# A graph layer on one core: a ring of twenty gather buffers, and 44 instead of 40 columns a step copied on the chip

## The chip, the cores and the metric

The kernel runs on one core of a Trainium2 chip. A core has five engines that run side by side: TensorE (PE, with its weight load shown apart as PEld), VectorE (DVE), ScalarE (ACT), GpSimd (POOL) and SyncE (SP, which here issues DMAs). Each engine has a sequencer that takes its instructions in program order; engines meet through semaphores. The metric is the device time of one execution in microseconds (us), lower is better.

## The reference, cut to what matters

A graph of 12500 nodes (64 features) and 212500 edges (32 features), the edges sorted by destination. For each edge a small network is applied to the source node, the destination node and the edge; messages are summed by destination; a second network updates each node, followed by a residual and a layer norm.

```python
def _L0_gnn_ref(nodes, row, col, edge_features, mW1, mb1, mW2, mb2, uW1, ub1, uW2, ub2):
    msg_in = jnp.concatenate([nodes[row], nodes[col], edge_features], axis=-1)
    messages = _mlp(msg_in, mW1, mb1, mW2, mb2)
    aggregated = jax.ops.segment_sum(messages, col, num_segments=nodes.shape[0])
    upd_in = jnp.concatenate([nodes, aggregated], axis=-1)
    return _mlp(upd_in, uW1, ub1, uW2, ub2)
x = _layernorm(x + _L0_gnn_ref(x, src, dst, edge_attr_32, ...), axis=-1)
```

`src` is random, so `nodes[row]` is a gather of 212500 rows of 256 bytes. `_mlp` is a matrix product, a ReLU and a second product.

## The kernel before, in words

Edges are worked on in 554 groups (`G`) of 384 edges, three tiles of 128. Since edges are sorted, all destinations of a group lie in a window of 32 consecutive nodes. All features of all nodes lie on the chip, transposed, in `own_xc` (64 partitions of features, one column a node, and a row of counts). The loop at the end of `ordered` runs over the groups; its body is one step `k`, and a step works on three groups at once:

- `turn(k)`: TensorE transposes the three gathered tiles of group k, together with their one-hot window matrix, into PSUM (line 341); ACT copies them to `own_st` (line 351), where the edge features have been loaded by SP.
- `hidden(k - 2)`: TensorE multiplies `own_st` with the weights `own_wm` (line 366), ACT applies the ReLU (line 377).
- `sums(k - 4)`: TensorE multiplies by the one-hot matrices, giving sums over the window of hidden vectors (line 394) and of edge counts (line 399). VectorE adds them into `agg` (line 406) and into the counts' row of `own_xc` (line 407), at a column held in a register.

TensorE's work of a step is issued in one run that waits once. PSUM buffers alternate, so a step's transposes need what ACT and VectorE did two steps before.

Source rows come in two ways. POOL gathers them from memory with one indirect DMA a tile (line 149, `gather`), `AHEAD` groups ahead of the loop, into a ring of `RING = AHEAD + 4` buffers `own_s`. A buffer may be written again when the transposes of the group before in it are done; before, both groups of a pair wait for the transposes of the pair's second group. But the first tile of some groups (those in `COPIED`) isn't gathered: its 128 columns are copied one by one out of `own_xc`, by VectorE and ACT, straight into `own_st` (`fetch`, lines 503 and 505; each copy is 64 partitions x 4 bytes). `COPIED` holds one group as soon as 128 more columns have been copied, from step 18 (`BEGIN`) up to ten steps before the last group. To copy a column, its address has to be in a register of the engine: a load instruction (line 490, `TENSOR_LOAD`) brings 8 or 12 addresses from `index` into registers at a time, then the copies follow. Addresses come in blocks of eight steps (`SPAN`), loaded by SP (`indexes`, line 467) and scaled on VectorE (`addresses`, line 473).

Other work on VectorE: `onehot(k + 2)` (line 329) each step; `places` once in four steps (a register load of four window starts, line 301, and four copies to `xw`, line 308); `windows` once in four steps (TensorE line 315, four copies to `own_wm`, line 320); and once in about 22.7 steps, when 512 nodes have all their sums, an `update`, cut into stages one step apart: TensorE and ACT apply the second network (lines 424 to 437), VectorE adds (428, 439), takes the statistics (443, 444) and normalizes (451, 454), SP stores.

The order on each engine is the program's order. VectorE, before, in a step: (places) - (update) - agg add - counts' add - (wm copies) - one-hot - load of 8 - 8 copies - load of 12 - 12 copies.

The lines that set the sizes:

```python
AHEAD = 4
RING = AHEAD + 4
VCOLS = (8, 12)
ACOLS = (12, 8)
COLS = sum(VCOLS + ACOLS)
SPAN = 8
```

The functions that the diff touches:

Of the kernel before, what the change touches and what calls it, by code (L numbers as in the profile page):

```python
# [15 lines left out]
ALU = mybir.AluOpType  # L16
ET = mybir.EngineType
# [6 lines left out]
D = 64  # L24
# [7 lines left out]
GE = TG * P  # L32
G = (E + GE - 1) // GE
SB = 4
AHEAD = 4
RING = AHEAD + 4
BLOCKS = 3
NW = 2 * SB
# [7 lines left out]
SHORT = 10  # L46
TIMES = 4
BEGIN = 18
CHECKED = 8
VCOLS = (8, 12)  # L50
ACOLS = (12, 8)
COLS = sum(VCOLS + ACOLS)
SPAN = 8


def tiles_of(g):

    n = min(GE, E - g * GE)
    return [min(P, n - j * P) for j in range((n + P - 1) // P)]
# [49 lines left out]
def ordered(ctx: ExitStack, tc: tile.TileContext, a, own, ok):  # L109
# [3 lines left out]
    nc = tc.nc  # L113
# [9 lines left out]
    xc = own.xc[: D + 2]  # L123
# [7 lines left out]
    loads, places_by, copy_by, relu_by, sums_by, wm_by, turn_by = ({} for _ in range(7))  # L131
# [3 lines left out]
    def after(first, *others):  # L135

        tc.declare_no_dep(first.ins, group="quiet", reason="waits for the last of a step")
        for i in others:
            tc.add_manual_dep(
                first.ins, i.ins.name,  # L140
                mybir.DependencyInfo(mybir.DependencyClass.Sync, mybir.DependencyReason.DATA),
                reason="the kernel's own rings",
            )
        return first

    def gather(g):
        s = own.s[g % RING]
        loads[g] = [
            nc.gpsimd.indirect_dma_start(  # L149
                out=s[:p, j, :D], out_offset=None, in_=x[:, :],  # L150
                in_offset=bass.IndirectOffsetOnAxis(
                    ap=src_sb[:p, g * TG + j : g * TG + j + 1], axis=0),
            )
            for j, p in enumerate(tiles_of(g)) if j or g not in columned
        ]
        for i in loads[g]:
            after(i, *([turn_by[g // 2 * 2 + 1 - RING]] if g >= RING else []))


    iota_i = const.tile([P, W], F32, name="iota_i")  # L160
# [3 lines left out]
    make_identity(nc, ident_t)  # L164
    for g in range(AHEAD):
        gather(g)
# [55 lines left out]
    for f, (g0, g1) in zip(firsts_f, halves):  # L222
        part = dlc[:, g0 * TG : g1 * TG].rearrange("p (g j) -> p g j", j=TG)
# [18 lines left out]
    agg = const.tile([P, NP], F32, name="agg")  # L242
# [49 lines left out]
    def columns(g):  # L292
        t, c = own.st[g // SB % BLOCKS], (g % SB) * GE
        return t, c, sum(tiles_of(g))
# [92 lines left out]
    def sums(g, ps):  # L387
        h, s = own.h[g % NH], own.s[g % RING]
        sizes = tiles_of(g)
        sg = ps[2][:, : TIMES * W].rearrange("p (t w) -> p t w", w=W)  # L390
        counted = ps[2][0:1, TIMES * W :][:, :W]
        did = []
        for j, p in enumerate(sizes):
            did.append(nc.tensor.matmul(  # L394
                sg, h[:p, j, :],
                s[:p, j, D:].unsqueeze(1).to_broadcast([p, TIMES, W]),
                start=j == 0, stop=j == len(sizes) - 1))
        for j, p in enumerate(sizes):
            did.append(nc.tensor.matmul(counted, own.one[:p], s[:p, j, D:],  # L399
                                        start=j == 0, stop=j == len(sizes) - 1))  # L400

        def add(step):
            sums_by[g] = step
            at = bass.ds(starts.pop(g), W)
            return [
                after(nc.vector.tensor_tensor(agg[:, at], sg[:, 0, :], agg[:, at], ALU.add), step),  # L406
                after(nc.vector.tensor_tensor(xc[D : D + 1, at], counted,  # L407
                                              xc[D : D + 1, at], ALU.add), step),
            ]

        return did, [*relu_by[g], *copy_by[g]], add

# [49 lines left out]
    def indexes(i):  # L462

        n = min(SPAN * COLS, P * len(COPIED) - i * SPAN * COLS)
        if n > 0:
            indices[i] = ixp.tile([1, SPAN * COLS], I32, name="index")
            nc.sync.dma_start(indices[i][:, :n], a["src_copied"][:, i * SPAN * COLS :][:, :n])

    def addresses(i):

        if i in indices:
            t = indices[i][:, : min(SPAN * COLS, P * len(COPIED) - i * SPAN * COLS)]
            nc.vector.tensor_scalar(t, t, 4.0, float(own.at), ALU.mult, ALU.add)

    def fetch(k):

        i, n = divmod(k - BEGIN, SPAN)
        if i < 0:
            return
        if n == 0:  # L480
            indexes(i + 1)
        if n == SPAN - 2:
            addresses(i + 1)
        c0 = (k - BEGIN) * COLS
        for engine, count in [*((ET.DVE, c) for c in VCOLS), *((ET.Activation, c) for c in ACOLS)]:
            count = min(count, P * len(COPIED) - c0)
            if count <= 0:
                return
            b = c0 - i * SPAN * COLS
            _, v = nc.values_load_multi_w_load_instructions(  # L490
                indices[i][0:1, b : b + count], engines=[engine],
                min_val=own.at, max_val=own.at + 4 * (N - 1),
                skip_runtime_bounds_check_because="a source is one of the nodes",
            )
            for q, at in zip(range(c0, c0 + count), v):
                g, c = COPIED[q // P], q % P
                t, first_c, _ = columns(g)
                o = t.bitcast(U8)[:D, 4 * (first_c + c) : 4 * (first_c + c + 1)]
                x_at = xc_bytes[:D, bass.ds(at - own.at, 4)]
                by = columns_by.setdefault(g, {})  # L500
                new = engine not in by
                if engine == ET.DVE:
                    by[engine] = nc.vector.tensor_copy(o, x_at)  # L503
                else:
                    by[engine] = nc.scalar.activation(o, x_at, AF.Copy)  # L505
                after(by[engine], *([hidden_by[g - BLOCKS * SB]] if new else []))
            c0 += count

    waiting = [(closes, update(base, p, n)) for base, p, n, closes in PLAN]
    now = []  # L510
# [13 lines left out]
    def step(*work):  # L524


        parts, used = [], []
        for part, g in work:
            ps, old = own.ps[g % 2], users[part][g % 2]
            parts.append((part, g, *part(g, ps)))  # L530
            used += old
        did = [i for p in parts for i in p[2]]
        after(did[0], *used, *(i for p in parts for i in p[3]))
        copies = None
        for part, g, *_ in parts:
            if part is sums:
                for b in [b for b in xws if (b - 1) * SB <= g][:1]:
                    last, copies = windows(b, own.ps[g % 2][2][:, (TIMES + 1) * W :][:, :H])
                    did.append(last)
        for i in did[:-1]:  # L540
            tc.no_tile_sem_insts.add(i.ins.name)
            tc.add_to_no_dep_group("quiet", i.ins)
        for part, g, _, _, follow in parts:
            if part is sums:
                step_update(g)
            users[part][g % 2] = follow(did[-1])
            if part is sums and copies:
                copies()
                users[part][g % 2] += [wm_by[b * SB + i] for i in range(min(SB, G - b * SB))]
# [6 lines left out]
    windows(0, ups.tile([H, CH], F32, name="u_ps")[:, :H], False)[1]()  # L556
    indexes(0)
    made = summed = 0

    for k in range(G):  # L560
        if k < BITS:
            bit(k)
        if k == CHECKED:
            addresses(0)
            combined()
            ordered_edges()
            early.close()
            up = ctx.enter_context(tc.tile_pool(name="upd", bufs=2))
        if k % SB == 2:
            inputs(k // SB + 2)  # L570
        if k % SB == 1:
            places(k // SB + 1)
        if k < G - SHORT:
            step((turn, k), *([(hidden, k - 2)] if k > 1 else []),
                 *([(sums, k - 4)] if k > 3 else []))
            made, summed = max(0, k - 1), max(0, k - 3)
        else:

            step((turn, k))
            for _ in range(2):  # L580
                if summed < made:
                    step((sums, summed))
                    summed += 1
            for _ in range(2):
                if made <= k:
                    step((hidden, made))
                    made += 1
        onehot(k + 2)
        fetch(k)
        if k + AHEAD < G:  # L590
            gather(k + AHEAD)
    while summed < G:
# [332 lines left out]
```

## Time and profile before

| | us |
|---|---|
| median of 3 runs | 1899.2 (1896.05 to 1899.49) |
| profiled execution | 1895.48 |
| its span, first to last instruction | 1893.5 |
| POOL busy | 1417.6 |
| VectorE busy | 1492.9 |
| ACT busy | 1550.7 |
| TensorE busy | 1361.4 |

The page gives, for a group of instructions, the line of the kernel, the engine, the operation, what it writes and reads, how many there were, then busy time and the mean duration of one in ns, then the idle time of the engine just before them and what ended most of it. "issue" as the end of idle time means that the engine waited for nothing that the profile shows, so the cause lies in its sequencer. Register loads, address arithmetic and waits are done by the sequencer and are not counted as busy; rows marked DVEq or ACTq are such. An idle time of an engine that doesn't set the pace costs nothing. The granted TensorE clock was 0.969 of full speed on average.

### The profile page before, as it was taken

What the parts mean: (1) busy time and instruction counts of PE and PEld (TensorE: products, weight loads), DVE (VectorE), ACT (ScalarE), POOL (GpSimd) and SP (SyncE); (2) the same over time, 40 slices, a digit from 0 to 9 for tenths busy, and PEclk for the clock granted to TensorE, in tenths of its full rate; (3) what the DMA queues carried; (4) which work ended last, traced back from release to release, by engine and by line L of the source; (5) the groups of instructions that cost most, each with busy time, mean ns of one, the idle gap of its engine ahead of it and who ended that gap; (6) DMA issues with size and microseconds to landing.
All of it is one profiled execution on the core that took longest, in us unless ns stands there. A gap on an engine that the chain in (4) does not pass through costs nothing. (4 is left out here: it accounts for less than half of the span.)

```text
span 1893.5 us, 58044 instructions
## 1 busy us (share of the span) xinstructions
PE 1361.4 (72%) x12209; PEld 1193.4 (63%) x12209; DVE 1492.9 (79%) x13761; ACT 1550.7 (82%) x11818; POOL 1417.6 (75%) x1504
## 2 busy tenths in 40 slices
PE   3776777677777777677676776877767767767777
PEld 3666666666666666666665666666666656666665
DVE  3578888778888788887888878878888887888873
ACT  3489889888888888988988888889888888898882
POOL 7777777777777777777777777777777777777774
PEclk9999999999999999999999999999999999999999
DMA  6322222222222222222222222222222222222221
GB/s 136 73 46 45 46 48 44 50 43 48 46 45 48 47 43 50 45 46 44 48 50 43 48 46 45 46 48 44 50 44 47 47 48 44 47 44 50 44 47 29
DMA packets 68440, 92.50 MB, mean 49 GB/s; under 512 B 30893, under 2 KB 38350, under 8 KB 68078
## 3 DMA queue, kind: packets, MB, share of 16 engines
q0 software_dynamic: 47904, 49.12, 14.7%
q1 hardware_dynamic: 19260, 39.12, 7.4%
q14 instruction: 260, 2.13, 0.4%
q8 instruction: 102, 1.67, 0.4%
q10 hardware_dynamic: 914, 0.46, 0.1%
HBM read 85.29 MB, written 3.20 MB: 47 GB/s over the span
## 5 line engine op out<-in xcount | busy, mean ns | idle before, releaser
L149 POOL DMA_INDIRECT own_s<-in_x,src_sb x1497 | 1416.8, 946 | 457.3 <-issue 407.5
L503 DVE COPY own_st<-own_xc 64x4 uint8 x10500 | 897.7, 190 | 231.0 <-issue 217.9
L505 ACT ACTIVATE own_st<-own_xc 64x4 uint8 x10492 | 1057.1, 194 | 18.2 <-issue 15.2
L341 PE MATMUL own_ps<-own_ident,own_s 128*96 128x128 f32 x1661 | 289.5, 285 | 496.0 <-DMA own_s<-in_x,src_sb 157.9
L341 PEld LDWEIGHTS own_ps<-own_ident,own_s 128*96 128x96 f32 x1661 | 169.3, 132 | 566.1 <-ACT own_h L377 240.7
L394 PE MATMUL own_ps<-own_s,own_h 128*128 128x128 f32 x3322 | 480.5, 283 | 4.1 <-ACT own_h L377 2.9
L366 PE MATMUL own_ps<-own_wm,own_st 128*128 128x128 f32 x3322 | 479.4, 283 | 0.0
L351 ACT ACTIVATE own_st<-own_ps 96x384 f32<-96x384 f32 (+2 forms) x718 | 293.2, 408 | 205.8 <-PE own_ps L399 104.7
L394 PEld LDWEIGHTS own_ps<-own_s,own_h 128*128 128x128 f32 x3322 | 432.6, 199 | 6.3 <-ACT own_h L377 4.7
L366 PEld LDWEIGHTS own_ps<-own_wm,own_st 128*128 128x128 f32 x3322 | 432.1, 199 | 1.4 <-issue 0.5
L377 ACT ACTIVATE own_h<-own_ps 128x384 f32<-128x384 f32 x553 | 263.9, 477 | 16.0 <-PE own_ps L366 16.0
L399 PE MATMUL own_ps<-own_s,own_one 128*1 128x32 f32 x3322 | 190.1, 194 | 0.0
L320 DVE COPY own_wm<-own_ps 32x128 f32<-32x128 f32 x550 | 156.9, 285 | 5.6
L399 PEld LDWEIGHTS own_ps<-own_s,own_one 128*1 128x1 f32 x3322 | 114.5, 84 | 69.4 <-issue 6.2
L329 DVE TENSOR_TENSOR own_s<-iota,dlc 128x96 f32<-128x96 f32 x554 | 142.4, 258 | 14.3 <-issue 0.2
L406 DVE TENSOR_TENSOR agg<-own_ps,agg 128x32 f32 x554 | 105.1, 190 | 59.5 <-PE own_ps L399 25.9
L407 DVE TENSOR_TENSOR own_xc<-own_ps,own_xc 1x32 f32 x554 | 101.2, 183 | 30.6 <-PE u_ps L425 11.4
L308 DVE COPY xw<-own_xc 66x32 f32 x554 | 73.0, 207 | 15.5 <-DMA own_xc<-in_xT 9.8
L315 PE MATMUL own_ps<-w1b,xw 66*128 66x128 f32 (+1 forms) x276 | 69.1, 333 | 0.0
L446 ACT ACTIVATE rstd<-mv,eps 128x4 f32<-128x4 f32 (+1 forms) x25 | 7.4, 297 | 55.3 <-DVE mv L444 55.3
L437 PE MATMUL u_ps<-u,u 128*128 128x64 f32 (+1 forms) x196 | 50.1, 399 | 0.5 <-ACT u L427 0.5
L437 PEld LDWEIGHTS u_ps<-u,u 128*128 128x128 f32 (+1 forms) x196 | 47.1, 324 | 2.2 <-ACT u L427 0.9
(62 smaller groups left out, 276.7 us busy)
## 6 DMA issues: line engine op xcount, KB each, us to landing
own_st<-in_efT SPq DMA_DIRECT2D x138, 192.0 KB
own_s<-in_x,src_sb POOLq DMA_INDIRECT x1497
xin<-in_x SPq DMA_DIRECT2D x24, 128.0 KB
out<-o SPq DMA_DIRECT2D x24, 128.0 KB
own_xc<-in_xT SPq DMA_DIRECT2D x12, 179.2 KB
index<-in_src_copied SPq DMA_DIRECT2D x65, 1.2 KB
dlc_i<-in_dst_cols SPq DMA_DIRECT2D x1, 831.0 KB
own_xc<-in_xT SPq DMA_DIRECT2D x4, 179.5 KB
```

The lines of the kernel that those rows point to most:

```text
L149: nc.gpsimd.indirect_dma_start(out=s[:p, j, :D], out_offset=None, in_=x[:, :], in_offset=bass.IndirectOffsetOnAxis(ap=src_sb[:p, g * TG + ...
L320: c = nc.vector.tensor_copy(wm[g % NW][D : D + W, :], wp[i * W : (i + 1) * W, :])
L329: places_by[g] = nc.vector.tensor_tensor(own.s[g % RING][:, :, D:], iota.unsqueeze(1).to_broadcast([P, TG, W]), dlc[:, g * TG : (g + 1) * ...
L341: nc.tensor.transpose(xt[:, j * P : j * P + p], s[:p, j, :], ident[:p, :p])
L351: after(nc.scalar.activation(t[r, c : c + n][:, m], xt[r, m], AF.Copy), step)
L366: nc.tensor.matmul(pre[:p, j, :], t[:, c + j * P : c + j * P + p], wm[g % NW], start=True, stop=True)
L377: relu_by[g] = [nc.scalar.activation(h, pre, AF.Relu)]
L394: did.append(nc.tensor.matmul(sg, h[:p, j, :], s[:p, j, D:].unsqueeze(1).to_broadcast([p, TIMES, W]), start=j == 0, stop=j == len(sizes) - 1))
L399: did.append(nc.tensor.matmul(counted, own.one[:p], s[:p, j, D:], start=j == 0, stop=j == len(sizes) - 1))
L406: after(nc.vector.tensor_tensor(agg[:, at], sg[:, 0, :], agg[:, at], ALU.add), step),
L503: by[engine] = nc.vector.tensor_copy(o, x_at)
L505: by[engine] = nc.scalar.activation(o, x_at, AF.Copy)
```

## The change

Two things. The ring of gather buffers has 20 groups instead of 8, gathers are issued 16 groups ahead instead of 4, and each group waits for its own predecessor in the ring. And VectorE copies 24 columns a step instead of 20, in three loads of eight instead of one of eight and one of twelve; the three blocks stand apart: the first between the agg add and the counts' add, the second after the counts' add (and wm copies), the third after the one-hot. With ACT's 20 these are 44 columns a step, so 180 tiles instead of 164 are copied and 1481 instead of 1497 are gathered. `fetch` takes the numbers of the parts that it is to do; the loads of indices and the scaling of addresses come behind the copies of their step. `between` is a list that hands the first block to `add`; where no add takes it (the first steps), it runs right after the step.

```diff
-AHEAD = 4
+AHEAD = 16
 RING = AHEAD + 4
-VCOLS = (8, 12)
+VCOLS = (8, 8, 8)
@@ gather
-            after(i, *([turn_by[g // 2 * 2 + 1 - RING]] if g >= RING else []))
+            after(i, *([turn_by[g - RING]] if g >= RING else []))
@@ sums, add
-            return [
-                after(nc.vector.tensor_tensor(agg[:, at], sg[:, 0, :], agg[:, at], ALU.add), step),
-                after(nc.vector.tensor_tensor(xc[D : D + 1, at], counted,
-                                              xc[D : D + 1, at], ALU.add), step),
-            ]
+            a = after(nc.vector.tensor_tensor(agg[:, at], sg[:, 0, :], agg[:, at], ALU.add), step)
+            if between:
+                between.pop()()
+            return [a, after(nc.vector.tensor_tensor(xc[D : D + 1, at], counted,
+                                                     xc[D : D + 1, at], ALU.add), step)]
@@ fetch
-    def fetch(k):
+    def fetch(k, *parts):
         i, n = divmod(k - BEGIN, SPAN)
         if i < 0:
             return
-        if n == 0:
-            indexes(i + 1)
-        if n == SPAN - 2:
-            addresses(i + 1)
-        c0 = (k - BEGIN) * COLS
-        for engine, count in [*((ET.DVE, c) for c in VCOLS), *((ET.Activation, c) for c in ACOLS)]:
+        all_parts = [*((ET.DVE, c) for c in VCOLS), *((ET.Activation, c) for c in ACOLS)]
+        for part in parts:
+            engine, count = all_parts[part]
+            c0 = (k - BEGIN) * COLS + sum(c for _, c in all_parts[:part])
...
-            c0 += count
@@ the loop
+    between = []
...
         if k < G - SHORT:
+            between.append(lambda: fetch(k, 0))
             step((turn, k), *([(hidden, k - 2)] if k > 1 else []),
                  *([(sums, k - 4)] if k > 3 else []))
             made, summed = max(0, k - 1), max(0, k - 3)
+            if between:
+                between.pop()()
+            fetch(k, 1)
...
         onehot(k + 2)
-        fetch(k)
+        if k < G - SHORT:
+            fetch(k, *range(2, len(VCOLS + ACOLS)))
+            if k >= BEGIN and (k - BEGIN) % SPAN == 0:
+                indexes((k - BEGIN) // SPAN + 1)
+            if k >= BEGIN and (k - BEGIN) % SPAN == SPAN - 2:
+                addresses((k - BEGIN) // SPAN + 1)
         if k + AHEAD < G:
             gather(k + AHEAD)
```

## The prediction, on record before the result

> **What bounds the kernel now.** I read the page first (engine totals, costliest groups), then the waits of POOL, then the instructions of the lines the change touches, and last VectorE alone in order of time.
>
> ```profile
> PE 1361.4 (72%) x12209; PEld 1193.4 (63%) x12209; DVE 1492.9 (79%) x13761; ACT 1550.7 (82%) x11818; POOL 1417.6 (75%) x1504
> ...
> L149 POOL DMA_INDIRECT own_s<-in_x,src_sb x1497 | 1416.8, 946 | 457.3 <-issue 407.5
> L503 DVE COPY own_st<-own_xc 64x4 uint8 x10500 | 897.7, 190 | 231.0 <-issue 217.9
> ```
>
> No engine is at 100%, but POOL's 75% misleads. Its 1497 gathers are 1416.8 us busy and 457.3 us idle just before them: 1874.1 us, 1.252 us each. Its waits say what that idle time is:
>
> ```profile
> POOL own_s L149 <- issue: 407.5, 1337, 0.3
> POOL own_s L149 <- DMA own_s<-in_x,src_sb: 36.6, 120, 0.3
> POOL own_s L149 <- PE own_ps L399: 10.1, 33, 0.3
> ```
>
> The longest gap in each row is 0.3 us, the same whoever "ended" it. So POOL issues gathers end to end for 1874 of 1893.5 us and waits for nobody. That is one bound: 16 gathers fewer are worth 16 x 1.252 = 20.0 us, if nothing else takes over.
>
> What could take over is VectorE. Its column copies have 218 us of "issue" before them, and the reason is another row, the register loads of line 490, which are sequencer work and counted busy nowhere:
>
> ```profile
> L490 DVEq TENSOR_LOAD <-index x1050: 591/843/1118, 80.5 to 1844.6; - x175
> ...
> L301 DVEq TENSOR_LOAD <-start_i x139: 340/344/594, 13.8 to 1863.6; - x139
> ```
>
> Half of the 1050 load 8 values, half 12: the minimum 0.591 us is the eight, the median 0.843 us the twelve. With 0.344 us for the four values of line 301 that is 0.0625 us a value and 0.09 us a load. VectorE in order of time:
>
> ```profile
> 905.56 0.26 DVE L329 TENSOR_TENSOR own_s<-iota,dlc 128x96 f32<-128x96 f32 x1
> 906.04 0.69 DVE L503 COPY own_st<-own_xc 64x4 uint8 x8 [0.23 <-issue]
> 907.21 1.16 DVE L503 COPY own_st<-own_xc 64x4 uint8 x12 [0.48 <-issue]
> 908.11 0.26 DVE L406 TENSOR_TENSOR agg<-own_ps,agg 128x32 f32 x1
> ...
> 910.74 0.17 DVE L406 TENSOR_TENSOR agg<-own_ps,agg 128x32 f32 x1
> ...
> 914.59 0.19 DVE L406 TENSOR_TENSOR agg<-own_ps,agg 128x32 f32 x1
> ...
> 917.59 0.19 DVE L406 TENSOR_TENSOR agg<-own_ps,agg 128x32 f32 x1
> ...
> 920.54 0.33 DVE L406 TENSOR_TENSOR agg<-own_ps,agg 128x32 f32 x1
> ...
> 923.17 0.20 DVE L406 TENSOR_TENSOR agg<-own_ps,agg 128x32 f32 x1
> ```
>
> See two things. From the first of eight copies to the first of twelve it is 1.17 us, though the copies keep the engine busy for only 0.69. 1.17 - 0.843 = 0.33 us is what the sequencer takes to issue eight copies and to turn to the load; then the load runs, and only then come more copies. Load and issue do not overlap: the sequencer is a second, serial resource. And a step without other VectorE work is exactly that resource's sum: 908.11 to 910.74 is 2.63 us, of which 0.591 + 0.843 load, 0.33 issue the eight, about 0.45 the twelve (a fixed part and a part per copy), and 0.42 is left for the address arithmetic and the other three instructions. A cycle of four steps (line 301's load, four xw copies and four wm copies come once in it) takes 923.17 - 910.74 = 12.43 us, 3.11 a step. POOL needs on average 1874.1 / 554 = 3.38 a step. VectorE is thus only some 8% quicker than POOL, and part of that margin goes into the update of 512 nodes every 22.7 steps.
>
> **The change part by part.** The sums are made against the profiled execution: 1893.5 us span, 1895.5 us in all; the median shown is 1899.2, 3.7 us above.
>
> *Fewer gathers.* 128 columns at 44 a step instead of 40 copy 180 tiles, not 164: 1481 gathers, POOL done 20.0 us earlier if it never waits.
>
> *Four more columns and a third load on VectorE.* Loads of 8+12 become 8+8+8: 3 x 0.591 - 1.434 = +0.34 us. Three blocks of eight at 0.591 + 0.33 = 0.92 are 2.76 us; with the 0.42 that is left, 3.18 us for a plain step instead of 2.63. Spreading the blocks (after the agg add, after the counts' add, after the one-hot) hides a load behind those adds on the engine (0.18 to 0.26 us each), but the sequencer still does all three in a row with everything else. On the engine alone four copies more are only 4 x 0.0855 (897.7 / 10500) = 0.34 us.
>
> *The cycle of four.* Before, 12.43 - 4 x 2.63 = 1.91 us belong to places and windows. The sequencer's part of it is 0.344 for the load, about 0.5 for four address computations and copies, 0.16 for issuing four wm copies: 1.0. The other 0.9 is the queue being full behind the wm copies (4 x 0.285 us). After, the engine is idle about 0.8 us of each plain step and has caught up before them, so part of that 0.9 goes. Ends: 4 x 3.18 + 1.0 = 13.7 and 4 x 3.18 + 1.9 = 14.6. I take 14.2.
>
> *The update.* The fetching steps run from 81.2 to 1846.3 us (the copies' first and last start): 1765 us, 524 steps or 131 cycles. 131 x 12.43 = 1628 leaves 137 us over 23 updates, 5.9 us each: the wait of y for TensorE, the statistics' chain, and waits for gathers. After, the waits for TensorE and gathers shrink, since TensorE's step is done early and the ring is full; the chain of y and eight statistics (0.42 + 4 x 0.20 + 4 x 0.18, some 1.8 us with gaps) stays, and the sequencer can't run past it. Ends 1.8 and 5.9; I take 3.0, nearer the chain, since the waits are what a VectorE-bound kernel loses.
>
> *Ring of twenty, single waits.* Gathers may run 20 groups ahead of the transposes instead of 8, each with its own wait. POOL waits for nothing now, so this frees nothing on POOL; it takes away TensorE's 157.9 us of waiting for gathers, which only matters where POOL is late. A wait costs POOL nothing (the gap is 0.3 us with or without one). Twelve groups more are issued ahead of the loop, on a POOL that is already busy from 2.9 us on: the first 81 us stay. In the last steps, gathers lie ready; from the last copy to the end it is 47.2 us now, paced by gathers to 1875.7; after, the steps' own rhythm of 2.7 us (agg at 1872.47, 1875.04, 1877.74) gives about 43.
>
> *What moves.* The counts' add now stands 0.9 us behind the agg add. TensorE needs it two steps later (the buffers alternate), and a step leaves TensorE about 1 us of slack: nothing. The index DMA on SP and the address arithmetic (0.37 us, once in eight steps) move behind the copies of the same step and are used two steps or more later: nothing. ACT does the same 20 copies and sixteen more split copies of transposes: about 0.2 us each, on an engine with 343 us idle: nothing.
>
> *Sum.* 81 + 131 x 14.2 + 23 x 3.0 + 43 = 81 + 1860 + 69 + 43 = 2053 us span, 2055 in all, and 2059 on the median's scale: 8.4% slower. With the low ends 81 + 1795 + 41 + 43 = 1960, with the high ends 81 + 1913 + 136 + 47 = 2177.
>
> **The rivals.**
>
> *POOL stays the bound* (faster). If VectorE's step with everything stays under POOL's new 1481 x 1.252 / 554 = 3.35 us, the time is 1899.2 - 20.0 = 1879. For it: VectorE shows 400 us idle, the added engine time is 2100 x 0.0855 = 180, and the deeper ring lets POOL run through the updates. It decides at a cycle of about 13.0 us (12.43 + four times 0.13); the loads alone add 4 x 0.34 = 1.36. Against it stands the 1.17 us between blocks. [...]
>
> *Only the engine's time counts.* The spread loads hide, and a step grows by four copies, 4 x 0.0855 = 0.34: cycle 13.8, with updates at 3.0: 81 + 1808 + 69 + 43 = 2001, 2007 on the median's scale. For it: loads do sit in front of idle engine time. Against: in the plain step the engine is not what is full.
>
> *Nothing is absorbed.* Wm copies and updates cost what they do now: 2177, 2183 on the median's scale. For it: a full queue may stall the sequencer the same way with loads between.
>
> **How the numbers follow.** Forecast (sequencer sum with part of the stalls gone, 1990 to 2130): 0.70. Engine's time only (1960 to 2010): 0.13. Nothing absorbed (2130 to 2185): 0.09. POOL-bound: 0.06. The remaining 0.02 is no change within 0.2%, which is about what a measurement of this kernel can tell. Faster 0.06, same 0.02, slower 0.92. The range 1960 to 2140 leaves out POOL-bound and most of the case above.
>
> **What would show it.** In the changed kernel's profile: 1572 VectorE loads, all near 0.59 us; plain steps of about 3.2 us from agg add to agg add and cycles of four near 14; POOL with real waits (gaps far above 0.3 us, ended by TensorE, since the ring is full); TensorE's waits for gathers near zero, for VectorE's one-hot and adds more; VectorE still with idle time called issue, not full. It is wrong if POOL's gaps stay at 0.3 us to the end, or if a plain step is below 2.9 us: then loads do run beside issue when adds lie between.

## The result and the profile after

The changed kernel takes 2139.72 us (median of 4 runs, 2138.34 to 2140.88) where the kernel before takes 1898.1 us on the same chip: a ratio of 1.127, with a 95% interval of 1.125 to 1.129. It is 12.7% slower. The forecast was 2059 us, 8.4% slower, with a range from 1960 to 2140. The side and the bound were right, but the loss was half as large again as forecast. That the time lies in the range at all is luck: it is 0.3 us inside the upper end, two of the four runs are above it, and it lies in the band of the rival "nothing is absorbed" (2130 to 2185), not in the forecast's own (1990 to 2130). The profiled execution has a span of 2136.9 us, and the working below goes by that span against the 2053 us that the sum gave.

First the page of the changed kernel: the engines' busy time, then its two costliest groups (busy time, mean ns of one, idle time just before them and what ended most of it).

```profile
PE 1491.7 (70%) x12209; PEld 1305.9 (61%) x12209; DVE 1673.3 (78%) x15837; ACT 1558.5 (73%) x11806; POOL 1401.8 (66%) x1488
...
L149 POOL DMA_INDIRECT own_s<-in_x,src_sb x1481 | 1401.0, 946 | 652.6 <-issue 369.8
L501 DVE COPY own_st<-own_xc 64x4 uint8 x12576 | 1119.3, 185 | 336.2 <-issue 262.9
```

No engine is fuller than before; POOL and ACT are emptier. VectorE shows 78%, where it showed 79% before. Next POOL's waits in the changed kernel (total us, times, longest us):

```profile
POOL own_s L149 <- issue: 369.8, 1192, 2.4
POOL own_s L149 <- PE own_ps L399: 207.0, 158, 5.3
POOL own_s L149 <- PE own_ps L315: 49.8, 49, 4.8
```

Before, no gap between two gathers was above 0.3 us. Now there are waits of up to 5.3 us, and the two rows that name TensorE hold 257 us: the ring is full, and POOL waits until TensorE has emptied a buffer. POOL is no longer the bound. The bound now shows only in rows that no engine's busy time contains, the register loads of VectorE (line 488 here, 490 before; duration in ns: least, median, most):

```profile
L488 DVEq TENSOR_LOAD <-index x1572: 591/595/852, 79.7 to 2085.6; - x197
```

1572 loads of 0.595 us, 935 us in all; before it was 525 of eight values and 525 of twelve, 753 us. And VectorE alone, in order of time (start us, duration us), for two plain steps:

```profile
937.42 0.17 DVE L405 TENSOR_TENSOR agg<-own_ps,agg 128x32 f32 x1
937.94 0.67 DVE L501 COPY own_st<-own_xc 64x4 uint8 x8 [0.35 <-issue]
938.64 0.18 DVE L408 TENSOR_TENSOR own_xc<-own_ps,own_xc 1x32 f32 x1
939.03 0.69 DVE L501 COPY own_st<-own_xc 64x4 uint8 x8 [0.21 <-issue]
939.63 0.24 DVE L329 TENSOR_TENSOR own_s<-iota,dlc 128x96 f32<-128x96 f32 x1
939.99 0.97 DVE L501 COPY own_st<-own_xc 64x4 uint8 x8
940.88 0.17 DVE L405 TENSOR_TENSOR agg<-own_ps,agg 128x32 f32 x1
...
944.14 0.17 DVE L405 TENSOR_TENSOR agg<-own_ps,agg 128x32 f32 x1
```

The three blocks of eight start 1.09 and 0.96 us apart though eight copies are busy for only 0.67: each waits for its own load. From add to add it is 3.46 and 3.26 us here. Over the fetching part, from the address arithmetic of one agg add to that of the next, the sequencer's own rows give a median of 3.12 to 3.20 us for a plain step (2.57 to 2.65 before). A cycle of four in which VectorE has no work of an update takes 14.75 us on average (12.53 before). Below, "cycle" is always this mean.

The span grew by 243 us. The 131 cycles of four take 131 x (14.75 - 12.53) = 291 us more. What is left of the fetching part, the updates, shrank from 1765 - 131 x 12.53 = 124 us to 2006 - 131 x 14.75 = 74 us, 50 less. The start and the end together take 2 us more. So the whole loss is in VectorE's ordinary steps; the updates gave a little back.

### The profile page after: what moved, and what is told of

Its sections match the earlier page's. It is cut to its first block, busy times and chain, and to the rows that moved or that the text cites. A ratio compares the mean times of both kernels' runs of the same rounds, so it can differ in the third digit from the quotient of the medians.

```text
span 2136.9 us, 60851 instructions
## 1 busy us (share of the span) xinstructions
PE 1491.7 (70%) x12209; PEld 1305.9 (61%) x12209; DVE 1673.3 (78%) x15837; ACT 1558.5 (73%) x11806; POOL 1401.8 (66%) x1488
## 5 line engine op out<-in xcount | busy, mean ns | idle before, releaser
L149 POOL DMA_INDIRECT own_s<-in_x,src_sb x1481 | 1401.0, 946 | 652.6 <-issue 369.8
L501 DVE COPY own_st<-own_xc 64x4 uint8 x12576 | 1119.3, 185 | 336.2 <-issue 262.9
L341 PE MATMUL own_ps<-own_ident,own_s 128*96 128x128 f32 x1661 | 314.1, 303 | 610.7 <-ACT own_st L503 213.2
L341 PEld LDWEIGHTS own_ps<-own_ident,own_s 128*96 128x96 f32 x1661 | 179.3, 139 | 687.3 <-ACT own_st L503 224.0
L394 PE MATMUL own_ps<-own_s,own_h 128*128 128x128 f32 x3322 | 535.8, 305 | 4.1 <-ACT own_h L377 3.6
L366 PE MATMUL own_ps<-own_wm,own_st 128*128 128x128 f32 x3322 | 520.9, 299 | 0.0
L394 PEld LDWEIGHTS own_ps<-own_s,own_h 128*128 128x128 f32 x3322 | 486.4, 220 | 6.2 <-ACT own_h L377 5.2
L366 PEld LDWEIGHTS own_ps<-own_wm,own_st 128*128 128x128 f32 x3322 | 472.9, 214 | 2.2 <-issue 0.5
L399 PE MATMUL own_ps<-own_s,own_one 128*1 128x32 f32 x3322 | 199.8, 200 | 0.0
L399 PEld LDWEIGHTS own_ps<-own_s,own_one 128*1 128x1 f32 x3322 | 121.1, 86 | 78.7 <-issue 25.7
L405 DVE TENSOR_TENSOR agg<-own_ps,agg 128x32 f32 x554 | 108.4, 196 | 47.4 <-PE own_ps L399 23.8
```

Source lines behind the costliest of these rows:

```text
L149: nc.gpsimd.indirect_dma_start(out=s[:p, j, :D], out_offset=None, in_=x[:, :], in_offset=bass.IndirectOffsetOnAxis(ap=src_sb[:p, g * TG + ...
L341: nc.tensor.transpose(xt[:, j * P : j * P + p], s[:p, j, :], ident[:p, :p])
L366: nc.tensor.matmul(pre[:p, j, :], t[:, c + j * P : c + j * P + p], wm[g % NW], start=True, stop=True)
L394: did.append(nc.tensor.matmul(sg, h[:p, j, :], s[:p, j, D:].unsqueeze(1).to_broadcast([p, TIMES, W]), start=j == 0, stop=j == len(sizes) - 1))
```

## The experiments

Theory: as in the forecast, VectorE's sequencer is a serial resource and loads and issue add up in it; and, beyond the forecast, the stall behind the wm copies stays. The extra load and that stall make the loss. Rivals: the ring or its single waits do it; the engine's own time for the added copies does it; the order of the blocks does it.

**The ring alone.** The kernel before, with the ring of twenty and single waits only.

```diff
-AHEAD = 4
+AHEAD = 16
-            after(i, *([turn_by[g // 2 * 2 + 1 - RING]] if g >= RING else []))
+            after(i, *([turn_by[g - RING]] if g >= RING else []))
```

> The kernel before with the ring of twenty and single waits alone. Theory (POOL's issue paces the kernel before and waits for nobody; the loss comes from VectorE's sequencer): no change, 1893 to 1902 us, POOL's gaps still 0.3 us at the longest. Rival (the deeper ring costs something of its own, by waits or by earlier gathers): over 1920 us. Rival (it lets POOL run through the updates): under 1885 us.

Measured: 1896.05 us against 1897.44, ratio 0.9996 (0.9987 to 1.0005). POOL's waits with the ring alone:

```profile
POOL own_s L149 <- issue: 333.7, 1095, 0.3
POOL own_s L149 <- DMA own_s<-in_x,src_sb: 89.9, 295, 0.3
POOL own_s L149 <- PE own_ps L399: 29.3, 96, 0.3
```

The names of what ended a gap change, the gaps do not: 0.3 us is the distance between two gathers, whoever is named. The time is the same. The ring is worth nothing where POOL is the bound.

**The columns alone.** The changed kernel with the old ring.

```diff
-AHEAD = 16
+AHEAD = 4
-            after(i, *([turn_by[g - RING]] if g >= RING else []))
+            after(i, *([turn_by[g // 2 * 2 + 1 - RING]] if g >= RING else []))
```

> The changed kernel with the old ring of eight and the old waits of pairs. Theory: the time of the changed kernel, 2125 to 2155 us, since VectorE is behind POOL either way. Rival (a good part of the 240 us is the ring's): under 2100 us.

Measured: 2135.62 us, ratio 1.1245 (1.1222 to 1.1268), cycle 14.71 us. The interval overlaps that of the changed kernel, so the columns are the whole of the loss. Where VectorE is the bound the ring is worth nothing either.

**The three blocks together.** The changed kernel, all parts of `fetch` behind the one-hot, as before the change.

```diff
-            between.append(lambda: fetch(k, 0))
...
-            fetch(k, 1)
...
-            fetch(k, *range(2, len(VCOLS + ACOLS)))
+            fetch(k, *range(len(VCOLS + ACOLS)))
```

(The `if between` in the loop stays; it finds nothing.)

> The changed kernel with its three blocks of eight together behind the one-hot, as the blocks of before were. Theory (the sequencer does the same loads and issues in a row wherever they stand): plain steps stay at 3.1 to 3.2 us, 2100 to 2160 us in all. Rival (spreading itself costs, since each load now stands in front of an idle engine): at least 100 us back, under 2040 us.

Measured: 2096.99 us, ratio 1.1067 (1.1033 to 1.1101), 3 us under the low end of what was expected. A plain step is the same, 3.17 us: the sequencer has the same sum to do in any order. The cycle is 14.49 instead of 14.75. Spreading the loads between other work thus bought nothing and cost 43 us, 131 x 0.26 = 34 of them in the cycle: less than the rival asked for (100 us), but not nothing as the forecast had it.

**The third block without its load.** Its eight copies read eight fixed columns, so that no address has to be loaded.

```diff
+            v = [own.at + 4 * j for j in range(count)]
+            if part != 2:
...
```

> The changed kernel without the register load of the third block: its eight copies read eight fixed columns, so the output is not the reference's. Engine work is the same. Theory (sequencer): 0.594 us of load and 0.08 of turning less a step, cycles of four at about 12.0 us, which puts VectorE ahead of POOL again: 1870 to 1915 us, paced by POOL's 1481 gathers. Rival (engine time of the copies): 2100 us or more.

Measured: 1913.48 us, ratio 1.0092 (1.0063 to 1.0122), with all 12576 copies. A plain step is 2.50 us, 0.68 less, and a cycle 12.78. POOL's waits, TensorE's waits for gathers, and VectorE's loads without the third load:

```profile
POOL own_s L149 <- issue: 313.0, 1027, 0.3
POOL own_s L149 <- DMA own_s<-in_x,src_sb: 114.9, 377, 0.3
...
PE own_ps L341 <- DMA own_s<-in_x,src_sb: 7.1, 6, 1.9
```

```profile
L490 DVEq TENSOR_LOAD <-index x1048: 591/595/853, 78.9 to 1860.6; - x175
```

Taking 524 loads away takes 226 us off (2139.72 - 1913.48), 0.43 each. A plain step gets 0.68 shorter; the step with the wm copies hardly does (4.83 us instead of 4.92), so only three steps of a cycle gain. The rival that only the engine's time counts falls: the copies are all still there. They take fixed addresses here, though, so a cost of taking an address from a register, if there is one, is left out with the load.

The time was in the expected range, but not for the expected reason: POOL does not set the pace here. Its last gather ends at 1856.1 us, 56.6 us before the end of the span (17.7 before), and TensorE waits for gathers only 7.1 us in all (157.9 before). With a ring of twenty POOL can run up to sixteen groups ahead without ever being stopped, so gaps of 0.3 us show only that nothing holds POOL up, not that the kernel waits for it. VectorE is still the slower of the two by a little: a step of the fetching part takes 3.40 us, and POOL needs 1481 x 1.252 / 554 = 3.35.

**The third block without its copies.** Meant as the counterpart: the load stays, the eight copies behind it are left out.

```diff
+            if part == 2:
+                continue
             for q, at in zip(range(c0, c0 + count), v):
```

> The changed kernel with the third block's load but without its eight copies, so those columns are not brought and the output is not the reference's. Theory: only the issue of eight copies goes, 0.24 to 0.33 us a step: 1960 to 2030 us, slower than the run without the load though 0.57 us of engine time a step is gone. Rival (engine time): as fast as or faster than the run without the load, under 1915 us.

Measured: 1878.41 us, ratio 0.9907 (0.9879 to 0.9936). Read alone, this speaks for the rival, that copies cost and loads do not. But the loads of this kernel are:

```profile
L488 DVEq TENSOR_LOAD <-index x1048: 591/596/849, 78.7 to 1821.5; - x175
```

They are 1048, not 1572. With nobody reading the registers, the load was taken out as well. The run therefore left out both and doesn't tell them apart. It gives something else: with VectorE out of the way POOL is the bound again, and here the kernel does wait for it:

```profile
PE own_ps L341 <- DMA own_s<-in_x,src_sb: 62.0, 60, 2.4
```

Its last gather ends 20.4 us before the end of the span, and the time is 17 us under that of before on the same chip (1895.83), near the 20 us that 16 gathers at 1.252 us are worth. The forecast's rival "POOL stays the bound" (1879 us) was the right time for a kernel in which those columns cost VectorE nothing.

**The third block with its load and one copy.** The last of the eight copies keeps the load alive; seven are left out.

```diff
-            for q, at in zip(range(c0, c0 + count), v):
+            for q, at in list(zip(range(c0, c0 + count), v))[-1 if part == 2 else 0 :]:
```

> The changed kernel with the third block's register load kept alive by one copy, its other seven copies left out, so those columns are not brought and the output is not the reference's. Theory: seven issues at 0.03 us go and the load stays, plain step 2.97 us, cycles of four at 13.8: 1990 to 2050 us. Rival (the engine time of the copies counts, 0.5 us a step): under 1920 us.

Measured: 2016.75 us, ratio 1.0624 (1.0605 to 1.0644). Its loads and copies:

```profile
L488 DVEq TENSOR_LOAD <-index x1572: 591/595/842, 78.9 to 1961.3; - x197
```

```profile
L501 DVE COPY own_st<-own_xc 64x4 uint8 x8908 | 851.7, 188 | 381.7 <-issue 281.8 <-DVE agg L405 27.5 <-ACT own_st L503 12.2
```

Here VectorE makes 3668 copies fewer than the changed kernel and 1592 fewer than the kernel before, and the time is still 6.2% above before. Beside the run without the third load (all copies, two loads: 0.9% above) this decides against the engine's time, by which it should have stayed under 1920 us: the load is the larger part, 226 us against 123 for seven copies. The copies are worth something because issuing them is sequencer work too (a plain step is 2.97 instead of 3.18 us, 0.03 a copy).

**One wm copy instead of four.** Of the four copies to `own_wm` in a cycle only the first is made.

```diff
+                if i == 0 or b < 2:
                     c = nc.vector.tensor_copy(wm[g % NW][D : D + W, :], wp[i * W : (i + 1) * W, :])
```

> The changed kernel with one of the four wm copies in each cycle (the other three weights are left stale, so the output is not the reference's). Theory (the cycle came out 0.46 us longer than forecast because the sequencer stands before a full queue behind the wm copies): the stall of about 0.55 us and three issues of 0.03 go from each of 131 cycles: 2045 to 2075 us. Rival (nothing stands behind them): three issues only, 2120 us or more.

Measured: 2043.07 us, ratio 1.0776 (1.0723 to 1.0829), 2 us under the low end. Plain steps are unchanged, 3.12 to 3.18 us; the step with the wm copies falls from 4.92 to 4.23 us, and the cycle from 14.75 to 14.04. Issuing three copies takes the sequencer only some 0.1 us, so most of these 0.69 us is a stall behind the copies. It is best seen in the changed kernel with both engines, TensorE and VectorE, in order of time (lines of other engines left out):

```profile
944.14 0.17 DVE L405 TENSOR_TENSOR agg<-own_ps,agg 128x32 f32 x1
...
944.68 0.66 DVE L501 COPY own_st<-own_xc 64x4 uint8 x8 [0.37 <-issue]
...
945.37 0.18 DVE L408 TENSOR_TENSOR own_xc<-own_ps,own_xc 1x32 f32 x1
945.48 1.18 DVE L320 COPY own_wm<-own_ps 32x128 f32<-32x128 f32 x4
...
946.68 0.80 DVE L501 COPY own_st<-own_xc 64x4 uint8 x8
947.54 0.26 DVE L329 TENSOR_TENSOR own_s<-iota,dlc 128x96 f32<-128x96 f32 x1
947.71 0.68 DVE L501 COPY own_st<-own_xc 64x4 uint8 x8
947.90 0.50 PE L341 MATMUL own_ps<-own_ident,own_s 128*96 128x128 f32 x3 [2.27 <-ACT own_st L503]
```

The eight copies of the second block can start only when the wm copies end, at 946.66, while their load was done at 945.99: the gap from the end of the second load to the start of the third is 0.71 us in this step and 0.36 in a plain one, and these are the medians over all steps too. Then the third load starts late, and the engine has nothing to catch up with.

**Two loads of twelve, spread.** The same 24 columns with one load less.

```diff
-VCOLS = (8, 8, 8)
+VCOLS = (12, 12)
```

> The changed kernel with the same 24 columns in two loads of twelve instead of three of eight. Theory: one load's fixed 0.09 us and 0.08 us of turning to it are saved in each of 524 steps, 90 us: 2030 to 2070 us. Rival (engine time counts, and the engine does the same copies): 2120 us or more.

Measured: 2123.86 us, ratio 1.1201 (1.1181 to 1.1221). This missed by more than 50 us and lies where the rival had put it (the engine does the same copies, 2120 us or more). The plain step is as computed, 3.02 us; but the mean over all steps of the fetching part is 3.79 us, hardly below the changed kernel's 3.83, and the cycle is 14.42. Many steps are much longer than the median one. The next run tells the rival from the spreading: it keeps the copies and puts the blocks together.

**Two loads of twelve, together.** The two edits above in one.

```diff
-VCOLS = (8, 8, 8)
+VCOLS = (12, 12)
...
-            between.append(lambda: fetch(k, 0))
...
-            fetch(k, 1)
...
-            fetch(k, *range(2, len(VCOLS + ACOLS)))
+            fetch(k, *range(len(VCOLS + ACOLS)))
```

> 24 columns in two loads of twelve, both blocks together behind the one-hot, ring of twenty. Theory (the 70 us that two loads of twelve should have saved in the spread form were lost because the counts' add and the wm copies wait behind a block, which lets TensorE idle and its clock fall): plain steps 3.0 us as in the spread form, but 1990 to 2040 us. Rival (something else holds the step near 3.8 us wherever the blocks stand): 2080 us or more.

Measured: 2023.24 us, ratio 1.0669 (1.0652 to 1.0685), plain step 3.01, cycle 13.88, mean step 3.61 us. With the same copies it is 100 us faster than the run before, so the rival of that run falls: it was the spreading. What VectorE waits for ahead of its agg add, first spread, then together:

```profile
DVE agg L405 <- PE own_ps L399: 39.4, 38, 3.6
```

```profile
DVE agg L405 <- PE own_ps L399: 25.4, 14, 4.5
```

So one load fewer is worth 74 us with the blocks together (2096.99 - 2023.24) and only 16 us with the blocks spread. In the spread form the counts' add and the one-hot come after a block of twelve and its load, so TensorE's run may come later and its sums too late for the next agg add. In three of four steps VectorE's sequencer stands 0.21 to 0.29 us on average ahead of its first load, where it stands 0.10 to 0.14 in the changed kernel. That chain was read from the rows and not tested, and the waits shown are only part of the 100 us; the granted clock differs a little as well (0.924 and 0.936), and whether it has a part stays open.

**One load of twenty-two, and one of twenty-four.** A try at a better kernel: the kernel before with the ring (its lines as above), and one load a step on VectorE.

```diff
...
-VCOLS = (8, 12)
+VCOLS = (22,)
...
```

> The kernel before with the ring of twenty and 22 columns on VectorE in one load instead of 20 in two. Theory: the load saved (0.09 + 0.08 us) pays for two columns (0.06 + 0.03 us each), so a plain step stays at 2.63 us, POOL stays the bound, and eight gathers fewer give 10 us: 1885 to 1892 us. Rival (VectorE's longer cycles after one load take over): 1897 us or more.

Measured: 2940.78 us, ratio 1.5506 (1.5485 to 1.5527), over 1000 us above what either theory gave. VectorE's loads:

```profile
L490 DVEq TENSOR_LOAD <-index x525: 602/2072/5211, 79.2 to 2888.1; - x175
```

The loads of a full step alternate between 1.82 and 4.94 us. With 22 + 20 columns a step, blocks begin 168 bytes apart, which is not a multiple of 16; every other step starts 8 bytes off one. Even the shorter of the two is longer than the 1.47 us that 0.09 + 22 x 0.0625 gives.

```diff
...
-VCOLS = (8, 12)
+VCOLS = (24,)
...
```

> As the run with 22 columns, but 24 in one load. Theory: plain step 2.82 us, cycles of four at about 13.2, with updates 1930 to 1990 us, VectorE the bound by a little. Rival (POOL stays the bound): 1879 us, 20 us under before.

Measured: 2087.04 us, ratio 1.1009 (1.0989 to 1.1028), 97 us above the upper end of what was expected. VectorE's loads, and VectorE in order of time:

```profile
L490 DVEq TENSOR_LOAD <-index x524: 1596/1602/1857, 79.0 to 2031.9; - x175
```

```profile
934.08 0.20 DVE L406 TENSOR_TENSOR agg<-own_ps,agg 128x32 f32 x1
934.34 0.18 DVE L407 TENSOR_TENSOR own_xc<-own_ps,own_xc 1x32 f32 x1
934.55 0.26 DVE L329 TENSOR_TENSOR own_s<-iota,dlc 128x96 f32<-128x96 f32 x1
935.41 1.86 DVE L503 COPY own_st<-own_xc 64x4 uint8 x24 [0.60 <-issue]
937.19 0.17 DVE L406 TENSOR_TENSOR agg<-own_ps,agg 128x32 f32 x1
```

The load is what 0.0625 us a value makes it. The step is not: about 3.1 us instead of the 2.82 expected, with a cycle of 14.33 instead of 13.2. After its load the sequencer needs 1.12 us until it is past 24 copies, against 0.33 for eight and 0.45 for twelve. The twelve copies more take it 0.67 us, 0.056 each, nearer to the 0.071 us from copy to copy on the engine than to the 0.03 us of an issue: this block of 24 goes in part at the engine's pace. How many of its copies do, no run shows.

**The same loads, 8 bytes further on.** The kernel before, with its block of addresses moved by two values and nothing else.

```diff
-            indices[i] = ixp.tile([1, SPAN * COLS], I32, name="index")
+            indices[i] = ixp.tile([1, SPAN * COLS + 8], I32, name="index")[:, 2 : SPAN * COLS + 2]
```

> The kernel before, with the block of addresses moved by two elements (8 bytes) in its buffer and nothing else. Why: in the run with 22 columns the loads whose block began 8 bytes off a multiple of 16 took 0.2 us a value (4.94 us for 22 on VectorE, 1.76 and 2.6 us for 8 and 12 on ACT) and the others 0.0625. Theory (the start of the block matters): loads of 8 and 12 take about 1.85 and 2.7 us on VectorE, a step 5.7 us, 3300 to 3600 us in all. Rival (it was the odd length of 22): 1893 to 1902 us.

Measured: 3447.84 us, ratio 1.8182 (1.813 to 1.8235). Its loads on VectorE:

```profile
L490 DVEq TENSOR_LOAD <-index x1050: 1837/2412/2739, 79.5 to 3390.7; - x175
```

Eight values go from 0.59 to 1.84 us and twelve from 0.84 to about 2.7, only by where the block begins; ACT's loads get as much longer (0.55 to 1.75 us and 0.78 to 2.59). That settles the long loads of the run with 22 columns. It also raises the disputed cost by itself: with the same instructions as before, VectorE's two loads take 3.1 us a step more, a plain step takes 5.7 instead of 2.6 us, and the kernel is 82% slower.

## Why the prediction was right, and where it was short

*POOL bounds the kernel before, VectorE's sequencer is close behind it.* Right. The ring alone moved nothing (ratio 0.9996), and with VectorE relieved the time went to 1878 us, 17 us down on the same chip, by POOL's 16 gathers. The sign that the forecast named for POOL (gaps of 0.3 us to the end) can't tell by itself with a ring of twenty, as the run without the third load shows.

*A plain step becomes 3.18 us: three loads of 0.591, three issues of 0.33, 0.42 for the rest.* Right: 3.12 to 3.20. That load and issue add up was the step on which the forecast stood. Leaving one load out shortens the step by 0.68 us while all copies stay. But right behind each load of the index block stand copies that take their addresses from it, in every run: whether the sequencer stands still during a load, or only these copies wait for their addresses, no run tells apart.

*The cycle: "the engine is idle about 0.8 us of each plain step and has caught up before them, so part of that 0.9 goes", 14.2 us.* Wrong, and the main miss. It measured 14.75, and 14.75 - 4 x 3.18 = 2.03 us beside the plain steps, against 12.53 - 4 x 2.63 = 2.01 before: nothing was absorbed. Three things were mistaken in this step. The idle engine did not help a sequencer that had no slack: the wm copies take the engine 1.18 us in a row, the block behind them doesn't start before they end, and the next load isn't reached until that block has begun. That is what the trace shows of the forecast's full queue: in 130 of the 131 steps with wm copies the third load starts 0.02 to 0.04 us after the first copy of that block, where in a plain step it is 0.27 us (median). The stall (0.71 - 0.36, and 0.35 at the counts' add less the 0.14 for issuing the four copies) is 0.56 us. The gap of 0.71 us comes in nearly every cycle now, and in the run with the blocks together too, where the one-hot stands between, so it is not the place right behind the wm copies that makes it; before, some half of the cycles had it (0.70 instead of 0.32 us). Why it was rarer there no run shows. And about 0.35 us of the 0.9 was never a stall: it is a pause of the sequencer that comes once in 128 instructions, about once a cycle, in both kernels. The error is 0.55 x 131 = 72 of the 84 us by which the sum was short.

*The updates: 23 x 3.0.* Right, a little low: (2006.5 - 131 x 14.75) / 23 = 3.2 us each, where it was 5.4 before. 5 us. The range that had been taken, 1.8 to 5.9, was wide, so that it came so near is in part luck.

*The end: 43 us.* It was 50.1 us from the last copy, where it was 47.2 before; the last steps did not go at the rhythm that was taken for them. 7 us. With 72 + 5 + 7 the 84 us are accounted for.

*Spreading moves nothing.* The forecast gave the order of the blocks no price. With blocks of eight it costs 43 us, with blocks of twelve 100. Part of this stands in the 14.75 above. Of the signs that were named for TensorE, its waits for gathers did go to near zero (157.9 us before, 7.9 after). Its longer waits for VectorE's one-hot did not come as a row of that name: TensorE's run is put down to ACT in the profile, 213 us ahead of line 341. But of its 418 idle stretches above 0.2 us that end at line 341, 406 end 0.07 to 0.13 us after a one-hot has finished (180 of 414 before), as at 947.90 above, where the one-hot ends at 947.80. So the one-hot most likely was the one that came last, and the row's name was wrong.

*The rivals.* "POOL stays the bound" needed a cycle of 13.0 us; it was 14.75. "Only the engine's time" fell with the run that keeps all copies and loses a load. "Nothing is absorbed" (2183 us) was right on the cycle and wrong on the updates, and lies 43 us above the time; the forecast's 2059 lies 81 below. The time lies in that rival's band, which had been given one chance in eleven, so the step of the forecast that set it apart from this rival, the absorbing of the stall, failed.

## What to carry to other kernels

When an engine shows "issue" ahead of many small instructions, add up its sequencer's own rows (register loads, address arithmetic, issue) as a resource of its own: here that sum gave the plain step within 0.06 us, while the engine's busy share stood at 79% before and 78% after a loss of 12.7%. Idle time of the engine was no credit against a full sequencer here (2.03 us of a cycle beside the plain steps, 2.01 before), so a stall measured before should be carried over whole unless a row shows what would remove it. An instruction whose result nobody reads may be taken out, as the third load was here (1048 loads instead of 1572), so look at the counts in the profile before concluding anything from a run that leaves its reader out. And where a ring lets a producer run far ahead, a producer without gaps need not be the bound (without the third load POOL's gaps stayed at 0.3 us, and its last gather ended 56.6 us before the end): look at whether its consumer waits for it, and at how long before the end it is done.

## What the runs showed that was not expected

- The time of a register load went by where its block begins. From a multiple of 16 bytes it takes 0.34 us for four values, 0.59 for eight, 0.84 for twelve, 1.60 for 24; 8 bytes off it takes 1.84 for eight and 4.94 for 22, about 0.2 us a value instead of 0.0625. A load of 22 that began on such a multiple took 1.82, more than one of 24, so the length seems to matter too; no run tests that alone. Nothing in the kernel's text shows it; two columns fewer a step cost 854 us (2940.78 against 2087.04).
- VectorE's sequencer pauses for about 0.35 us once in 128 instructions of its program, always at the same place in the 128. The profile has 19682 of its instructions in the changed kernel and 17084 before, so there are some 20 pauses more, 7 us. What the pause is, no run shows.
- The granted TensorE clock is lower in the runs in which TensorE is busy for less of the span: 0.969 before (72% busy), 0.896 after (70%), 0.768 with 22 columns (61%), 0.661 with the shifted addresses (60%). The same matmuls of line 341 take longer on average: 285, 303, 363 and 374 ns. No run shows that this set a time here: VectorE's waits for TensorE's sums of line 399 are 23.8 us after the change and 25.9 before it.
